# Result tiles summed by halves, row tiles six steps apart, one adapter product four steps later

## The chip, the cores and the metric

The kernel runs on one core of one Trainium2 chip. The metric is the device time of one execution in microseconds (us), lower is better. Times of several executions are given by their median. TensorE (PE) does the matrix products, PEld are its weight loads, VectorE (DVE), ScalarE (ACT) and GpSimd (POOL) do elementwise work, and SyncE (SP) issues all the DMAs that matter here.

## The reference, cut to what matters

Eight sequences of 512 rows, 1024 wide, all float32. The last two matrix products of each sequence, each followed by a layer norm and a residual sum, are what this case is about:

```
x = x + layernorm(attention(layernorm(x)) @ Wo)          # "projection"
x1 = layernorm(x)
y = x1 @ weight.T + bias + (x1 @ A[adapter]) @ B[adapter]  # adapter for some sequences only
x = x + layernorm(y)                                     # "last stage"
```

The adapter product (rank 16, three adapters side by side and masked) is added to y.

## The kernel before, in words

**Products.** Every 512 x 1024 by 1024 x 1024 product is done by a Strassen-Winograd scheme of two levels: seven groups (`GROUPS`, L51) of seven products each (`SUBS`), so 49 products of one sequence. One product is one **step** of the schedule. It is two matmuls of 128x256 (with float32 they show as four records) and takes 0.864 us when nothing is in the way, in the last stage 0.43 us more where an adapter product is added to the same PSUM tile. The sequences are counted q = 0 to 15: 0 to 7 are the projection, 8 to 15 the last stage. So q begins at step base = 49 q, and the stage runs from about 1690 us to the end of the span. The first three groups of q = 0 are done in the stage before.

**The order of work is written by hand.** `at(tick, fn)` puts a piece of work on a step; `run` (L176) goes through a step in this order: work marked "pe", then the product of the step and the drain of the product before it (`fill`, L375), then all other work in the order in which it was put there. Each engine does its instructions strictly in that order. For one q, `plan_right` (L1149) is put down before the sums of result tiles, and those before `plan_rows` (L1181); rows of q - 1 that fall into the steps of q come before all of them.

**A group's drain.** A group's result is one tile of 2 x 512 columns; half j holds the rows of one row tile. In `Group.drain` (L339) ACT copies product P1 (slot 1 of the seven) to `p1`, DVE adds accumulator b to it (`u2`). After P7 (slot 5) DVE runs three adds of 128x256: `p1` plus b, then two result quarters (from accumulators c and d). P2 (slot 6) gives the quarter that completes **half 0**, copied by ACT one step later. P3 of the group is run in slot 2 of the next group, into the same accumulator c, and its drain, one step later, completes **half 1**. So the P3 matmul in slot 2 must wait until the DVE adds that follow P7 have read accumulator c. With the last group of a sequence (steps 42 to 48, result tile `A`), that is: product P7 in step 47, its DVE adds in step 48, and the P3 matmul in step 51, two steps into the next sequence.

**Sums of result tiles.** Tiles c11, c21, c12, c22, U and A are then summed (`combine`, L358). DVE does a whole tile in one instruction (128x1024), POOL does two of 128x512. Before, the steps within a sequence are: 18 c11+=A (DVE), 38 c21+=c12 (POOL), 45 U+=A, 46 c22+=U (DVE), 47 c21+=U (POOL), 48 c12+=c22, 52 c22+=A (DVE).

**Rows.** `plan_rows` takes four row tiles t through their layer norm: load, statistics on DVE, `norm` on ACT, `add_row` on POOL (L1106), store; in the projection also a second layer norm (x1), its transposes on DVE (`turn_x1`, L1115, 0.7 us each) and the store of x1 in DRAM (`store_x1`, eight small DMAs a tile), which is read back eight sequences later.

**Right operands.** `plan_right` loads R11, R21, R12, R22 of the next sequence (SP) and forms T1, T2, T4, T3 in three instructions each (`sum_right`, L275: 128x512, 128x512, 128x768). In the projection all four are POOL's. For q >= 8 T1 and T3 are DVE's; there each R is also differenced (`sub_right`, L263), and `lora_in` (L1135) puts 16 short matmuls per half of the rows on PE, whose result DVE masks (`lora_keep`, L1144).

Of the kernel before, what the change touches and what calls it, by code (L numbers as in the profile page):

```python
# [18 lines left out]
B, S, E = 8, 512, 1024  # L19
# [11 lines left out]
ALL = slice(None)  # L31
# [101 lines left out]
def sandwich_kernel(  # L133
# [15 lines left out]
    nc = tc.nc  # L149
# [43 lines left out]
    def at(tick, fn, kind=None):  # L193
        events[tick].append((kind, fn) if kind else fn)
# [51 lines left out]
    def load_right(pool, q, n):  # L246

        g, h = int(n[1]) - 1, int(n[2]) - 1
        open_right(pool, q, n)
        if q < B:  # L250
            nc.sync.dma_start(out=RX[q, n], in_=attn[q][:, g, h])
            return
        for m in range(4):
            t, k = divmod(m, 2)
            nc.sync.dma_start(
                out=RX[q, n][:, m].rearrange("p c n -> p (c n)").rearrange("p (a m) -> p a m", a=4),
                in_=x1t[q - B][:, 2 * h + t, :, 2 * g + k, :],
            )
# [96 lines left out]
            elif p == "P3":  # L355
                add(self.dest(0, 1), t["u2"], "c")

    def combine(q, out, x, y, eng):  # L358
        for j in (ALL,) if eng is nc.vector else (0, 1):
            eng.tensor_tensor(C[q, out][:, j], C[q, x][:, j], C[q, y][:, j], op=ALU.add)  # L360


# [32 lines left out]
    def stats(key, srcs, step):  # L395
        small = env["small"]
        if step == 0:
            ln[key] = small.tile([P, 2, 6], F32, tag="bnst", name=f"bn_{key}")
        if step < 2:
            nc.vector.bn_stats(ln[key][:, step, :], srcs[step])  # L400
        if step == 1:
            mv = small.tile([P, 2], F32, tag="mv", name=f"mv_{key}")
            nc.vector.bn_aggr(mv, ln[key])
            ln[key] = mv
        if step == 2:
            mv = ln[key]
            sd = small.tile([P, 1], F32, tag="sd", name=f"sd_{key}")
            nc.scalar.activation(sd, mv[:, 1:2], AF.Sqrt, bias=eps, scale=1.0)
            ln[key] = mv, sd
        if step == 3:  # L410
            mv, sd = ln[key]
            rs = small.tile([P, 1], F32, tag="rstd", name=f"rstd_{key}")
            nc.vector.reciprocal(rs, sd)
            nb = small.tile([P, 1], F32, tag="nb", name=f"nb_{key}")
            nc.vector.tensor_scalar(nb, mv[:, 0:1], rs, -1.0, op0=ALU.mult, op1=ALU.mult)
            ln[key] = rs, nb

    def norm(key, dst, src):
        rs, nb = ln[key]
        nc.scalar.activation(dst, src, AF.Identity, bias=nb, scale=rs)  # L420
# [16 lines left out]
    dve, pool = nc.vector, nc.gpsimd  # L437
# [104 lines left out]
    for b in range(B):  # L542
        base = b * N2
# [46 lines left out]
    for n in range(8):  # L590
        base = min(n + 1, B - 1) * N2
# [71 lines left out]
    m = {}  # L663
# [225 lines left out]
    late = {k - (B * N2 + 4): events[k] for k in sorted(events)}  # L889
# [61 lines left out]
    for u in range(UQ + 1):  # L951
        for k in () if u in (0, UQ) else (4, 13, 22, 31) if u in (4, 5, 6) else (18, 26, 34) if u == 1 else (9, 19, 29):
            base = u * N2 + k
# [17 lines left out]
    AHEAD = 3 * NP  # L971
# [28 lines left out]
    for u in range(UQ + 1):  # L1000
        base = u * N2
# [14 lines left out]
        else:  # L1016
# [24 lines left out]
            for k in range(10, 57):  # L1041
                if k in (51, 56):
                    n = {51: "S2", 56: "S4"}[k]
# [14 lines left out]
    with ExitStack() as a:  # L1058
# [26 lines left out]
        def sub_ht(b):  # L1085
            t = hts[b]
            nc.gpsimd.tensor_tensor(t[:, 4:6], t[:, 0:2], t[:, 2:4], op=ALU.subtract)
            nc.gpsimd.tensor_tensor(t[:, 6:9], t[:, 0:6:2], t[:, 1:6:2], op=ALU.subtract)
# [3 lines left out]
        def halves(q, t):  # L1092
            h, j = divmod(t, 2)
            tags = (("c11", "c21"), ("c12", "c22") if q + 1 == NQ else ("c22", "c12"))[h]
            return [C[q, tag][:, j, :] for tag in tags]
# [12 lines left out]
        def store_rows(q, t):  # L1108
            for h, c in enumerate(halves(q, t)):
                dst = x1d[q][:, t, ts(h, HALF)] if q < B else out[q - B, ts(t, P), ts(h, HALF)]  # L1110
                nc.sync.dma_start(out=dst, in_=c)

        def turn_x1(q, t, g):

            nc.vector.transpose(  # L1115
                halves(q, t)[g].rearrange("p (a k n c) -> p k c a n", a=4, k=2, n=32),
                row[q, t][:, ts(g, HALF)].rearrange("p (k c a n) -> p k c a n", k=2, c=2, a=4),
            )

        def store_x1(q, t, g):  # L1120
            for a in range(4):
                nc.sync.dma_start(
                    out=x1t[q][:, t, a, ts(g, 2)].rearrange("(c e) k n -> e c (k n)", e=32),
                    in_=halves(q, t)[g][32 * a : 32 * a + 32].rearrange("e (c m) -> e c m", c=4),
                )
# [23 lines left out]
        def plan_right(q, base):  # L1149

            if q > 1:
                at(base + 6, next_roles)
            for n, k in (("R11", 10), ("R21", 17), ("R12", 24), ("R22", 31)):
                if q == 1 and n != "R22":
                    continue
                at(base + k, lambda n=n: load_right(gp, q, n))
                if q >= B:
                    at(base + k + 4, lambda n=n: sub_right(q, n, nc.gpsimd, slice(0, 3)))
            if q >= B:
                for h, k in ((0, 25), (1, 39)):  # L1160
                    at(base + k, lambda h=h: lora_in(q - B, h), "pe")
                    at(base + k, lambda ph, h=h: lora_keep(q - B, h, ph), "post")
                    for g in range(2):
                        at(base + k, lambda n=f"R{g + 1}{h + 1}": sub_right(q, n, nc.vector if h else nc.gpsimd, slice(3, 4)))
                at(base + 42, lambda: sub_ht(q - B))
            for n, k in (("T1", 40 if q == 1 or q >= B else 38), ("T2", 46 if q >= B else 45), ("T4", 52), ("T3", 63)):
                eng = nc.vector if q >= B and n in ("T1", "T3") else nc.gpsimd
                for m in range(3):
                    at(
                        base + k + (m if eng is nc.vector else 0),  # L1170
                        lambda n=n, m=m, eng=eng: sum_right(gp, q, n, eng, slice(m, m + 1)),
                    )
# [8 lines left out]
        def plan_rows(q, base):  # L1181

            for t in range(NT):
                k = base + 55 + 7 * t
                key = f"{'o' if q < B else 'y'}{q}_{t}"
                at(k, lambda t=t: load_row(q, t))
                for m in range(4):
                    at(k + m + m // 2, lambda t=t, m=m, key=key: stats(key, halves(q, t), m))
                for h in range(2):
                    at(k + 6 + h, lambda t=t, h=h, key=key: norm(key, halves(q, t)[h], halves(q, t)[h]))  # L1190
                    at(k + 8 + h, lambda t=t, h=h: add_row(q, t, h))
                at(k + 14, lambda t=t: store_rows(q, t))
                if q < B:
                    key = f"x{q}_{t}"
                    for m in range(4):
                        at(k + 14 + m + m // 2, lambda t=t, m=m, key=key: stats(key, halves(q, t), m))
                    for h in range(2):
                        at(k + 20 + h, lambda t=t, h=h, key=key: norm(
                            key, row[q, t][:, ts(h, HALF)], halves(q, t)[h]
                        ))  # L1200
                    for g in range(2):
                        at(k + 24 + g, lambda t=t, g=g: turn_x1(q, t, g))
                        at(k + 29 + g, lambda t=t, g=g: store_x1(q, t, g))

        def plan_last(q, base):

# [38 lines left out]
        for q in range(NQ):  # L1245
            base = q * N2
            if q + 1 < NQ:
                plan_right(q + 1, base)
            if q == B - 1:
                plan_left(base)  # L1250
            dve, pool = nc.vector, nc.gpsimd
            for k, e, res, l, r in (
                (18, dve, "c11", "c11", "A"), (38, pool, "c21", "c21", "c12"), (45, dve, "U", "U", "A"),
                (46, dve, "c22", "c22", "U"), (47, pool, "c21", "c21", "U"),
                (48, dve, "c12", "c12", "c22"), (52, dve, "c22", "c22", "A"),
            ) if q + 1 < NQ else (
                (18, dve, "U", "U", "A"), (31, dve, "c12", "c12", "U"), (33, dve, "U", "U", "c22"),
                (34, pool, "c22", "c22", "c12"), (39, pool, "c11", "c11", "A"),
                (45, dve, "c21", "c21", "c12"),
            ):  # L1260
                if base + k >= AHEAD:
                    at(base + k, lambda a=(q, res, l, r, e): combine(*a))
            if q + 1 < NQ:
                plan_rows(q, base)
            else:
                plan_last(q, base)
# [95 lines left out]
```

## Time and profile before

| | |
|---|---|
| median of 3 runs | 2483.34 us (2482.4 to 2485.61) |
| the profiled execution | 2482.47 us, of which the span of the trace is 2480.7 us |
| PE, DVE, POOL, ACT busy | 96%, 72%, 59%, 43% of the span |
| PE waits from 1690 us to the end | 23.8 us in 15 gaps |
| mean granted TensorE clock | 0.987 of full speed |

The page gives averages over stages with different limits, so the stage that is changed is read by itself. Groups of instructions are named by their line, engine, operation and tiles (out<-in); a helper has one line for many uses, so the tile names and shapes tell them apart. A wait "X <- Y" means that X's engine sat idle until Y was done. In the timeline an instruction's duration runs from its start on the engine to its end, so it holds any time in which the engine was held up inside it.

### The profile page before, as it was taken

To read this page: it belongs to the slowest core of one execution; us is meant where nothing else is said; L and a number is where in the kernel's file an instruction comes from. 1 tells how busy PE (TensorE), PEld (TensorE's weight loads), DVE (VectorE), ACT (ScalarE), POOL (GpSimd) and SP (SyncE) were. 2 spreads that over 40 slices of the span, in tenths; PEclk is the share of its full clock that TensorE was granted. 3 is DMA by queue.
4 is the path that set the end of the run, shared out by engine and by line. 5 is a ranking of instruction groups with operands and counts; after the bars stand their busy time and mean duration, and the time that the engine had idled before them with its cause. 6 is when DMAs were issued, how large, how long until landed. Compare 5 with 4: busy or idle time off the path is not lost.

```text
span 2480.7 us, 37119 instructions
## 1 busy us (share of the span) xinstructions
PE 2373.1 (96%) x11936; PEld 1868.7 (75%) x11936; DVE 1791.5 (72%) x3945; ACT 1060.3 (43%) x2685; POOL 1464.1 (59%) x1087
## 2 busy tenths in 40 slices
PE   6999999999999999999999999899999998999997
PEld 4787887886677777777777766458888877888886
DVE  8777767485857759586684856766898987766676
ACT  3323331025555555556555566762434333222223
POOL 3878875204463553736545363326787886777674
PEclk8999999999999999999999999899999999999999
DMA  7697787998899897988989896557778798444433
GB/s 262 197 302 248 243 269 235 346 296 266 269 307 276 256 342 236 326 282 288 333 262 328 265 312 214 169 196 267 230 207 250 201 280 220 126 130 124 115 111 119
DMA packets 505650, 601.82 MB, mean 243 GB/s; under 512 B 198417, under 2 KB 344849, under 8 KB 502898
## 3 DMA queue, kind: packets, MB, share of 16 engines
q1 hardware_dynamic: 505458, 599.46, 76.2%
q8 instruction: 96, 1.57, 0.3%
q14 instruction: 96, 0.79, 0.1%
HBM read 366.55 MB, written 199.23 MB: 228 GB/s over the span
## 4 chain that ended last, share of the span: by engine, by line
PE 66%; DVE 7%; DMA 5%; POOL 2%; ACT 2%; issue 1%; SPq 1%; ACTq 0%; POOLq 0%; DVEq 0%
PE accc_q_P L641 7%; PE accb_q_P L641 7%; PE acca_q_P L641 7%; PE accc_P L320 7%; PE accb_P L320 6%; PE acca_P L320 6%; PE s L752 6%; PE po L832 5%; PE ptp L811 5%; PE accd_P L320 3%; PE accd_q_P L641 3%; DMA attn<-opt 1%; PE ph L1135 1%; DMA R<-x1t 1%; ACT pr L797 1%
## 5 line engine op out<-in xcount | busy, mean ns | idle before, releaser
L783 ACT ACTIVATE pr<-pr,nm 128x128 f32<-128x128 f32 (+3 forms) x512 | 280.9, 550 | 171.9 <-DVE nm L773 171.7
L797 ACT ACTIVATE pr<-pr,rs 128x128 f32<-128x128 f32 (+2 forms) x500 | 245.2, 549 | 117.2 <-DVE rs L791 117.1
L773 DVE CUSTOM_DVE_ANT_0 pr<-s,mask 128x128 f32<-128x128 f32 (+3 forms) x512 | 224.4, 485 | 43.5 <-PE s L752 40.9
L641 PE MATMUL acca_q_P<-xs,ls 128*128 128x256 f32 x896 | 217.3, 385 | 0.8 <-issue 0.8
L641 PE MATMUL accc_q_P<-xs,ls 128*128 128x256 f32 x896 | 217.7, 386 | 0.0
L1106 POOL TENSOR_TENSOR c<-c,row 128x512 f32<-128x512 f32 x120 | 158.3, 1328 | 99.7 <-ACT c L420 84.0
L641 PE MATMUL accb_q_P<-xs,ls 128*128 128x256 f32 x896 | 216.3, 384 | 0.8 <-DVE u_q_P L116 0.8
L641 PEld LDWEIGHTS acca_q_P<-xs,ls 128*128 128x128 f32 x896 | 165.3, 190 | 49.9 <-issue 20.4
L641 PEld LDWEIGHTS accc_q_P<-xs,ls 128*128 128x128 f32 x896 | 165.8, 190 | 48.4 <-issue 20.8
L752 PE MATMUL s<-qk 64*128 64x128 f32 (+3 forms) x1024 | 194.5, 474 | 6.0 <-DVE nm L773 5.5
L641 PEld LDWEIGHTS accb_q_P<-xs,ls 128*128 128x128 f32 x896 | 165.4, 190 | 44.9 <-issue 6.9
L811 PE MATMUL ptp<-ident,pr 128*128 128x128 f32 x1280 | 178.4, 278 | 11.8 <-ACT pr L797 5.6
L275 POOL TENSOR_TENSOR T<-R,T 128x512 f32<-128x512 f32 (+1 forms) x96 | 174.0, 1839 | 24.0 <-PE accc_P L320 17.3
L811 PEld LDWEIGHTS ptp<-ident,pr 128*128 128x128 f32 x1280 | 147.2, 142 | 44.4 <-ACT pr L797 17.1
L567 POOL TENSOR_TENSOR wc_g<-wc_g 128x256 f32<-128x256 f32 (+1 forms) x120 | 125.9, 1068 | 80.0 <-DMA wc_g<-in_wqk_dram 76.7
L832 PE MATMUL po<-pT,v 128*64 128x512 f32 (+3 forms) x1024 | 158.1, 447 | 9.8 <-ACT pT L826 9.8
L832 PEld LDWEIGHTS po<-pT,v 128*64 128x64 f32 x1024 | 72.9, 138 | 102.3 <-issue 65.5
L683 POOL TENSOR_TENSOR B_q<-B_q,m 128x1024 f32<-128x1024 f32 x14 | 34.9, 2496 | 189.0 <-DVE B_q L680 189.0
L752 PEld LDWEIGHTS s<-qk 64*128 64x128 f32 x1024 | 73.2, 187 | 47.5 <-issue 28.7
L641 PE MATMUL accd_q_P<-xs,ls 128*128 128x256 f32 x448 | 108.7, 385 | 0.0
L826 DVE COPY pT<-ptp 128x384 f32<-128x384 f32 (+1 forms) x129 | 78.7, 615 | 38.1 <-PE ptp L811 38.1
L567 POOL TENSOR_TENSOR wc_wo<-wc_wo 128x256 f32<-128x256 f32 (+1 forms) x64 | 66.0, 1047 | 64.0 <-DMA wc_wo<-in_wo_dram 50.1
(1107 smaller groups left out, 5710.1 us busy)
## 6 DMA issues: line engine op xcount, KB each, us to landing
ls<-wqk SPq DMA_DIRECT2D x392, 256.0 KB, 5.1
xs<-xop SPq DMA_DIRECT2D x392, 256.0 KB, 5.3
R<-attn SPq DMA_DIRECT2D x32, 896.0 KB, 6.3
wqk<-wc_g SPq DMA_DIRECT2D x16, 1568.0 KB, 9.4
x<-in_x_dram SPq DMA_DIRECT2D x32, 512.0 KB, 9.6
v<-vd SPq DMA_DIRECT2D x64, 256.0 KB, 5.4
attn<-ops SPq DMA_DIRECT2D x16, 1024.0 KB, 8.1
row<-in_x_dram SPq DMA_DIRECT2D x32, 512.0 KB, 4.2
```

Source lines behind the costliest of these rows:

```text
L275: eng.tensor_tensor(RX[q, n][:, c], RX[q, x][:, c], RX[q, y][:, c], op=ALU.subtract)
L320: nc.tensor.matmul(acc, lhsT=stays, rhs=moving, start=(first and k == 0), stop=True, skip_group_check=True,)
L567: eng.tensor_tensor(out, x, y, op=op)
L641: nc.tensor.matmul(acc[:, :, w, :], lhsT=ls[:, k, w, :], rhs=xs_[:, :, k, :], start=(first and w == 0 and k == 0), stop=True, skip_group_c ...
L752: nc.tensor.matmul(ps[:, j, at : at + L], lhsT=qT[r, qb], rhs=kT[r, : qb + 1], start=True, stop=True,)
L773: nc.vector.tensor_tensor_reduce(out=v[:, j, :], in0=self.ps[qb][:, j, :], in1=work2["mask"][:, S - L :], scale=-1.0 / HD**0.5, scalar=3.0e38,
L783: nc.scalar.activation(v[:, j, :], v[:, j, :], AF.Exp, bias=nm[:, j : j + 1], scale=-1.0, accum_out=sm[:, j : j + 1],)
L797: nc.scalar.mul(v, v, rs[:, j : j + 1])
L811: nc.tensor.transpose(pt[:, n, :], self.pr[qb][:, j, ts(kb, P)], ident)
L826: copy(self.pT[j][:, : qb + 1, ts(qb, P)], self.pt[j][:, : qb + 1, :])
L832: nc.tensor.matmul(po[j * HD : (j + 1) * HD, kb * P :], lhsT=self.v[:, kb, ts(j, HD)], rhs=self.pT[j][:, kb, kb * P :], start=(kb == 0), s ...
L1106: nc.gpsimd.tensor_tensor(c, c, row[q, t][:, ts(h, HALF)], op=ALU.add)
```

## The change

Three things are done; the number of products and their order are the same.

1. The sums of result tiles of q = 0 to 14 are done by halves, each at its own step. Seven sums become fourteen instructions; on DVE 128x512 twice takes the place of 128x1024 once. c12+=c22 now comes in steps 44 and 47, ahead of the drain of step 48, and the first half of c21+=U ahead of T2 in POOL's order.
2. Row tile t starts at step base + 53 + 6 t, before at base + 55 + 7 t, and what comes from the store on is one step nearer to the row tile's start.
3. Only for the operands of q = 8 (in q = 7's steps): the second `lora_in` with its `lora_keep`, two `sub_right` and `sub_ht` is four steps later, T1 at step 45 and no longer 40, T2 at 48 and no longer 46.

```diff
-    def combine(q, out, x, y, eng):
-        for j in (ALL,) if eng is nc.vector else (0, 1):
+    def combine(q, out, x, y, eng, j=None):
+        for j in (j,) if j is not None else (ALL,) if eng is nc.vector else (0, 1):
             eng.tensor_tensor(C[q, out][:, j], C[q, x][:, j], C[q, y][:, j], op=ALU.add)
...
-                for h, k in ((0, 25), (1, 39)):
+                late = 4 * (q == B)
+                for h, k in ((0, 25), (1, 39 + late)):
...
-                at(base + 42, lambda: sub_ht(q - B))
-            for n, k in (("T1", 40 if q == 1 or q >= B else 38), ("T2", 46 if q >= B else 45), ("T4", 52), ("T3", 63)):
+                at(base + 42 + late, lambda: sub_ht(q - B))
+            for n, k in (("T1", 45 if q == B else 40 if q == 1 or q > B else 38), ("T2", 48 if q == B else 46 if q > B else 45), ("T4", 52), ("T3", 63)):
...
-                k = base + 55 + 7 * t
+                k = base + 53 + 6 * t
...
-                at(k + 14, lambda t=t: store_rows(q, t))
+                at(k + 13, lambda t=t: store_rows(q, t))
...
-                        at(k + 24 + g, lambda t=t, g=g: turn_x1(q, t, g))
-                        at(k + 29 + g, lambda t=t, g=g: store_x1(q, t, g))
+                        at(k + 23 + g, lambda t=t, g=g: turn_x1(q, t, g))
+                        at(k + 28 + g, lambda t=t, g=g: store_x1(q, t, g))
...
-            for k, e, res, l, r in (
-                (18, dve, "c11", "c11", "A"), (38, pool, "c21", "c21", "c12"), (45, dve, "U", "U", "A"),
-                (46, dve, "c22", "c22", "U"), (47, pool, "c21", "c21", "U"),
-                (48, dve, "c12", "c12", "c22"), (52, dve, "c22", "c22", "A"),
+            for ks, e, res, l, r in (
+                ((14, 18), dve, "c11", "c11", "A"), ((36, 38), pool, "c21", "c21", "c12"),
+                ((42, 45), dve, "U", "U", "A"), ((43, 46), dve, "c22", "c22", "U"),
+                ((44, 47), pool, "c21", "c21", "U"), ((44, 47), dve, "c12", "c12", "c22"),
+                ((50, 53), dve, "c22", "c22", "A"),
```

The steps of the second layer norm's statistics and `norm` move by the same one step. The sums of the last sequence (q = 15) keep their steps and sizes.

## The prediction on record

> **What bounds it.** I read the page first: PE is busy 96% of the span. So only PE's gaps can be won, and the stage from 1690 us on was asked by itself for what PE waits for (total us, times, longest):
>
> ```profile
> PE accc_P L320 <- DVE A L342: 14.5, 9, 1.9
> PE ph L1135 <- DMA R<-x1t: 4.4, 2, 3.7
> PE accb_P L320 <- DVE u_P L342: 2.6, 2, 2.1
> PE accc_P L320 <- DVE U L342: 1.3, 1, 1.3
> PE accb_P L320 <- POOL T L275: 1.0, 1, 1.0
> ```
>
> The first row is the P3 matmul of step 51, held by the DVE adds of step 48. The timeline places it: 1.91, 1.91, 1.91, 1.05, 1.92, 1.91 us at the ends of q = 1 to 6 (1754 to 1978 us), 1.25 at q = 7, the rest at q = 8 and in the last sequence. From q = 9 to 14 PE has no gap. A second cost hides in the windows cut at those matmuls (length, busy times, then granted clock):
>
> ```profile
> 1753.90:1800.10 46.20, 44.26 (x196) 38.34 (x196) 40.51 (x89) 18.65 (x38) 36.32 (x25) 0.96 0.81 236
> 1800.10:1844.70 44.60, 42.72 (x196) 37.07 (x196) 40.42 (x89) 18.75 (x38) 36.74 (x25) 1.00 0.70 211
> ```
>
> After the gap at 1754 the clock is halved for a while: 4% of 46.2 us, about 1.8 us lost. It happens after two of the five gaps of 1.9 us (q = 1 and 6), after the 2.07 us one (q = 7) and after the 3.7 us one, not after shorter ones.
>
> **Why DVE is late at step 48.** The timeline of the end of q = 5, DVE, POOL and PE:
>
> ```profile
> 1928.06 1.27 POOL L275 TENSOR_TENSOR T<-R,T 128x512 f32<-128x512 f32 x1
> 1928.13 2.28 DVE L360 TENSOR_TENSOR U<-U,A 128x1024 f32<-128x1024 f32 x1
> ...
> 1929.29 2.25 POOL L275 TENSOR_TENSOR T<-R,T 128x512 f32<-128x512 f32 x1
> ...
> 1930.45 2.17 DVE L360 TENSOR_TENSOR c<-c,U 128x1024 f32<-128x1024 f32 x1
> ...
> 1931.50 2.79 POOL L275 TENSOR_TENSOR T<-R,T 128x768 f32<-128x768 f32 x1
> 1932.55 0.41 DVE L342 TENSOR_TENSOR p_P<-accb_P,p_P 128x256 f32<-128x256 f32 x1
> 1932.99 0.42 DVE L342 TENSOR_TENSOR A<-accc_P,p_P 128x256 f32<-128x256 f32 x1
> ...
> 1933.47 0.92 PE L320 MATMUL accc_P<-wo_S,R 128*128 128x256 f32 x3 [1.92 <-DVE A L342]
> ```
>
> Read the ends. POOL's first T ends at 1929.33; DVE's U, begun at 1928.13, ends 1.08 us after that. POOL's next T, begun at 1929.29, ends at 1931.54, 1.13 us after U. c22 ends 1.08 us after that T. Alone, the DVE sum takes 1.22 us (q = 0) and the POOL one 1.27. So a DVE sum of two SBUF operands and a POOL sum **exclude each other and take turns**: each DVE instruction lets one POOL instruction pass, 1.13 us (128x512) or 1.68 (128x768). DVE's adds from PSUM (0.41), statistics (0.68) and transposes (0.70) don't lengthen. A DVE instruction of half size pays the same turn, as a 128x512 one shows:
>
> ```profile
> 2018.50 1.45 POOL L1106 TENSOR_TENSOR c<-c,row 128x512 f32<-128x512 f32 x1
> ...
> 2018.75 1.75 DVE L275 TENSOR_TENSOR T<-R,R 128x512 f32<-128x512 f32 x1
> ```
>
> 1.75 us: 1.20 until POOL's ended (2019.95), then 0.55. Alone it takes 0.65 (2045.33 us).
>
> **Part 1, the halves.** Before step 48's adds there were two big DVE sums (U, c22); now there are six half ones (U, c22, c12 twice), as c12+=c22 moves in front of that drain. What each lets pass decides.
>
> End of q = 5 in its own times: step 38 at 1920.17, 42 at 1923.62, 51 at 1931.4. Row tile 3's add_row is now at steps 30 and 31 and out of POOL's way, so T1 starts at 1920.4 (before 1921.36), and its third instruction ends at 1924.65. Then, in turns (0.53 for a DVE half, 1.13 or 1.68 for POOL): U half 0 to 1925.2, POOL's c21 half 1 to 1926.3, c22 half 0 to 1926.85, c21+=U half 0 to 1928.0, c12 half 0 to 1928.5, T2 to 1929.65, U half 1 to 1930.2, T2 to 1931.3, c22 half 1 to 1931.85, T2's 768 columns to 1933.55, c12 half 1 to 1934.1, two adds of step 48 (0.9) to 1935.0. The adds of steps 44 and 45 and two transposes (0.34 + 0.31 + 1.26) fit into the turns. PE wanted 1931.4: **a gap of 3.6 us where there was 1.92**. If T1 starts 1.2 us later, one POOL instruction takes the place of another, with the same end. After such a gap I count 0.1 for the restart and 0.8 times the halved clock's 1.8: 5.0 us a boundary. Six of them 30.0; before, 10.6 of gaps, 0.6 of restarts, two halved clocks 3.6, together 14.8. **+15.2.** From below: without turns (six at 0.62) DVE would be done at 1930.9, and the whole 14.8 is won.
>
> **The last stage** had no gap but little room. End of q = 11:
>
> ```profile
> 2252.45 2.17 DVE L360 TENSOR_TENSOR c<-c,U 128x1024 f32<-128x1024 f32 x1
> ...
> 2254.99 0.42 DVE L342 TENSOR_TENSOR A<-accc_P,p_P 128x256 f32<-128x256 f32 x1
> ...
> 2256.11 0.81 PE L320 MATMUL accc_P<-wf_S,R 128*128 128x256 f32 x3
> ```
>
> The adds are done 0.7 us before PE wants them. DVE's T1 ends at 2250.2, as before; then U half 0 to 2250.85 and c22 half 0 to 2251.45 without a turn, POOL's c21+=U half 0 to 2252.6, c12 half 0 to 2253.15, T2 to 2254.3, U half 1 to 2254.85, T2 to 2256.0, c22 half 1 to 2256.5, T2's 768 to 2258.2, c12 half 1 to 2258.75, the adds to 2259.65: **a gap of 3.5 us that was not there**, again 5.0 with its clock. q = 9 to 14: **+30.0**; q = 8, which had 2.9 of gaps there: **+2.1**. From below: without turns the adds end at about 2255.5, and nothing is lost.
>
> q = 0 has no rows in these steps, but T1 of q = 1 at step 40 stands in U's way: by the same turns 1.5 us of gap are new, and the 1.0 us for POOL's T4 goes, as half a c21 sum moves into an idle time of POOL's: **+0.5**. c11 in halves at steps 14 and 18 now meets two row tiles' statistics (steps 16 to 18): from 0 to 0.6 us in six sequences, **+1**. c22+=A (50, 53) comes behind the adds; DVE has room until step 55, so nothing; without that cover 0.5 per boundary.
>
> **Part 2, the rows.** No instruction is added; a row tile's ten DMAs, ACT's norms and POOL's adds stay as many, and ACT (some 18.7 of 45 us) and POOL have the room. What moves is SP's queue: the last eight x1 stores of q = 7 come at q = 8's steps 1 and 2, before at 7 and 8, where they stood right in front of R11's load for q = 9 (stores until 2043.1 us, load 2043.2). From 2036 to 2064 us the DMA queue is 96% busy, and PE waits 3.7 us for R21, with a halved clock behind it. Those stores held SP for 4.7 us (1.91 + 2.75), more than 3.7. Between nothing and 5.5 us won; I take all of it, as 4.7 is over 3.7: **-5.5**.
>
> **Part 3.** In q = 7's steps 0.67 us of waiting for R22 go. But `lora_keep` (0.54), two differences (0.41 alone) and T1's three (0.65, 0.65, 0.95 alone) move from steps 39 to 42 into 43 to 47, behind `lora_in` (2.0 us of PE), in front of the same drain. In us from step 42: the masks can't start before 2.95, c22 half 0 ends at 6.45, the add PE needs for step 47 at 6.8 (0.5 late), then, in turns, T1, U and c22's second halves, transposes and c12 to 15.75, the adds 16.6; step 51 wants them at 10.2. 0.5 + 6.4 + 1.8 = 8.7, before 0.67 + 2.07 + 1.25 + 1.8 + 0.2 = 6.0: **+2.7**, from -4 (turns missed) to +6 (R22 late too).
>
> **Sum:** 15.2 + 30.0 + 2.1 + 0.5 + 1.0 - 5.5 + 2.7 = +46.0 on the profiled execution's 2482.47 (span 2480.7 and 1.8 around it; 0.9 under the median): **2528.5 us**.
>
> [...]
>
> **Rivals.** *The halves pass without turns* (10%): the mechanism is the port's order at steps 42 to 47. For it speaks that U half 0 starts three steps earlier and that the first two halves of the last stage meet no POOL work; against it that T2 must run in just these steps (its buffer is free at step 45). With no turn the projection's chain ends 0.5 us before PE wants it. It decides from the second or third turn on: 2.4 us of delay bring the old gap of 1.92 back. Price: -14.8 - 2.9 - 5.5 - 2 (q = 7) - 1.0 = -26: **2456 us**. *The boundaries stay as they are* (5%): half of the turns are missed, DVE's earlier start pays for the others, and only R21's wait goes: **2477 us**. The forecast has 85%.
>
> **Range.** Own case: no halved clock -20, the last stage's gaps 2 us shorter -14; upward the clock always halved +5, R21's wait stays +5.5, c11 +2.6, q = 7 +3.3. 2494 to 2545, a little more for sums of them: 2492 to 2546 holds nearly all of 85%. A measurement tells some 0.2% (5 us) from no change; half of the second rival lies over that. Faster 13%, same 3%, slower 84%.
>
> **What would show it.** PE's row accc_P <- DVE A with some 15 entries and 45 to 55 us, longest 3 to 6.5, also in q = 9 to 14; DVE's L360 as 128x512, about 1.6 us in the mean though 0.65 alone; POOL's T2 between them one by one; the clock under 1.00 in most sequences of the stage; no wait for R<-x1t over 1 us. I am wrong if DVE's halves are near 0.7 us, or if two of them run with a POOL sum waiting.

## The result, and the profile after

| us | before | after |
|---|---|---|
| median of 4 runs each | 2482.87 (2478.72 to 2485.61) | 2548.95 (2546.74 to 2550.47) |
| the profiled execution, and its span | 2482.47, 2480.7 | 2548.88, 2547.1 |
| PE waits from 1690 us to the end | 23.8 | 60.3 |
| mean granted clock | 0.987 | 0.976 |

The changed kernel is slower by 2.7%: the ratio is 1.0272, 95% interval 1.0257 to 1.0288. The forecast was 2528.5 with a range of 2492 to 2546, so the sign and the place were foreseen and the size was not: 66.4 us in the profiles where 46.0 were forecast.

What PE waits for, from 1690 us to the end of the kernel after (total us, times, longest):

```profile
PE accc_P L320 <- DVE A L342: 53.0, 16, 5.9
PE accb_P L320 <- DVE u_P L342: 4.8, 8, 1.9
PE ph L1135 <- DMA R<-x1t: 1.4, 1, 1.4
```

The row that stood at 14.5 us with 9 entries has 53.0 with 16. That is the P3 matmul of step 51, now held at every boundary: 2.74 us at q = 0, 3.51 to 3.53 at q = 1 to 6, 5.90 at q = 7, 3.12 at q = 8, 3.11 at q = 9 to 14, and the last sequence's 1.49 as before. The row of R<-x1t falls from 4.4 to 1.4.

The end of q = 5 in the timeline of the kernel after, some lines of DVE, POOL and PE:

```profile
1951.54 0.81 DVE L360 TENSOR_TENSOR U<-U,A 128x512 f32<-128x512 f32 x1
...
1952.89 1.13 DVE L360 TENSOR_TENSOR c<-c,U 128x512 f32<-128x512 f32 x1
1953.43 2.25 POOL L275 TENSOR_TENSOR T<-R,T 128x768 f32<-128x768 f32 x1
1954.13 2.10 DVE L360 TENSOR_TENSOR c<-c,c 128x512 f32<-128x512 f32 x1
1956.16 0.41 DVE L342 TENSOR_TENSOR p_P<-accb_P,p_P 128x256 f32<-128x256 f32 x1
1956.60 0.42 DVE L342 TENSOR_TENSOR A<-accc_P,p_P 128x256 f32<-128x256 f32 x1
1957.08 0.80 PE L320 MATMUL accc_P<-wo_S,R 128*128 128x256 f32 x1 [3.53 <-DVE A L342]
```

Read the ends again. POOL's 768 columns of T2 start at 1953.43, when the second half of c22 is under way, and end at 1955.68. The second half of c12 starts on DVE at 1954.13 and ends at 1956.23, 0.55 us after POOL. It takes 2.10 us, of which 0.55 lie behind POOL's end (a half sum right after, at 1957.46 us, takes 0.69 in all). Only then come the two adds for which PE waits. This is the order that the forecast had, and its last turn.

The rest of the price is mostly in the clock. Two of the windows cut at the matmuls of step 51 (length, busy times, clock), one of the projection and one of the last stage, where before the clock was 1.00:

```profile
1858.20:1908.20 50.00, 45.82 (x197) 38.95 (x197) 44.07 (x94) 18.51 (x38) 35.65 (x25) 0.94 0.68 201
2185.00:2243.60 58.60, 55.50 (x260) 47.32 (x260) 40.63 (x78) 11.89 (x26) 38.95 (x33) 0.97 0.39 108
```

And the 3.4 us pieces around the gap at 1957 us:

```profile
1952.50:1955.90 3.40, 1.05 (x5) 0.57 (x3) 3.29 (x3) 0.30 (x1) 3.40 (x3) 1.00 0.67 134
1955.90:1959.30 3.40, 2.22 (x5) 1.85 (x6) 2.55 (x7) 0.37 (x1) 1.46 (x2) 0.50 0.90 264
1959.30:1962.70 3.40, 3.40 (x9) 2.69 (x8) 3.18 (x5) 0.00 (x0) 3.40 (x3) 0.50 0.16 65
1962.70:1966.10 3.40, 3.40 (x17) 2.96 (x17) 1.56 (x5) 0.57 (x2) 1.30 (x1) 1.00 0.00 0
```

For two whole pieces the clock is 0.50, and a PE that is busy all the time gets through 9 records where it gets through 17 in the next. Cut into such pieces, the stage after has fifteen halved stretches, ten of one piece and five of two; before it had four. Fourteen of the fifteen boundaries have one (only q = 8 has none), and the fifteenth follows a wait of 1.90 us at step 40 of q = 7.

### The profile page after: what moved, and what is told of

Its sections match the earlier page's. It is cut to its first block, busy times and chain, and to the rows that moved or that the text cites. A ratio compares the mean times of both kernels' runs of the same rounds, so it can differ in the third digit from the quotient of the medians.

```text
span 2547.1 us, 37198 instructions
## 1 busy us (share of the span) xinstructions
PE 2400.1 (94%) x11936; PEld 1883.4 (74%) x11936; DVE 1844.1 (72%) x4019; ACT 1056.6 (41%) x2685; POOL 1455.4 (57%) x1087
## 3 DMA queue, kind: packets, MB, share of 16 engines
q8 instruction: 96, 1.57, 0.3%
## 4 chain that ended last, share of the span: by engine, by line
PE 52%; DVE 15%; DMA 7%; POOL 4%; issue 3%; ACT 3%; SPq 1%; DVEq 0%; ACTq 0%; POOLq 0%
PE accc_q_P L641 6%; PE acca_q_P L641 6%; PE accb_q_P L641 6%; PE accc_P L320 5%; PE s L752 5%; PE po L832 5%; PE ptp L811 4%; DVE c L360 4%; PE accb_P L320 4%; PE acca_P L320 3%; PE accd_q_P L641 3%; PE accd_P L320 2%; DMA attn<-opt 1%; PE ph L1135 1%; DVE U L360 1%
## 5 line engine op out<-in xcount | busy, mean ns | idle before, releaser
L773 DVE CUSTOM_DVE_ANT_0 pr<-s,mask 128x128 f32<-128x128 f32 (+3 forms) x512 | 224.2, 484 | 41.1 <-PE s L752 39.0
L275 POOL TENSOR_TENSOR T<-R,T 128x512 f32<-128x512 f32 (+1 forms) x96 | 163.9, 1733 | 29.0 <-PE accc_P L320 13.4
L263 POOL TENSOR_TENSOR R<-R 128x256 f32<-128x256 f32 x96 | 77.6, 809 | 67.7 <-DMA R<-x1t 55.0
```

The costliest lines, as they stand in the source:

```text
L275: eng.tensor_tensor(RX[q, n][:, c], RX[q, x][:, c], RX[q, y][:, c], op=ALU.subtract)
L773: nc.vector.tensor_tensor_reduce(out=v[:, j, :], in0=self.ps[qb][:, j, :], in1=work2["mask"][:, S - L :], scale=-1.0 / HD**0.5, scalar=3.0e38,
```

## The experiments

My theory stayed that of the prediction: DVE's sums of two SBUF operands and POOL's sums take turns (before, at the end of q = 5, each ended 1.08 to 1.13 us after the other's), so work put in front of the drain of step 48 costs its own time and POOL's beside it. Its rivals were that the halving itself costs (twice as many instructions, twice as many turns), that another part of the change costs, and that the clock takes more than I gave it. Each ratio is to the kernel before, with its 95% interval.

**One part at a time: e1_halves, e2_rows, e3_late.** Each is the kernel before with one of the three parts of the diff, as printed above.

> The kernel before with part 1 alone (sums by halves at the changed steps; rows and adapter product as before). Theory (turns between DVE's half sums and POOL's sums hold up the adds of step 48): nearly all of the +66 us, 2535 to 2550 us, gaps of 3.4 to 3.6 us at the ends of q = 1 to 6 and of 3.0 to 3.2 at q = 9 to 14, each with a halved clock behind it. Rival (the rows, now packed, and the late adapter product make the time, a half sum costs only its start): 2483 to 2490 us, gaps under 2 us.

> The kernel before with part 2 alone (row tiles six steps apart). Theory: the gaps at the ends of q = 1 to 6 stay near 1.9 us, some 0.5 us at step 33 are new in each, the wait of 3.7 us for R21 at q = 8 gets shorter or goes: 2476 to 2487 us. Rival (the rows make the time): over 2510 us.

> The kernel before with part 3 alone (second adapter product of q = 8 four steps later, T1 at 45, T2 at 48). Theory: q = 7 alone changes, the gap at its end grows from 1.25 to 3 to 5 us, the wait for R22 goes: 2482 to 2489 us. Rival (it makes a good part of the time): over 2495 us.

- e1_halves: 2559.47 us, ratio 1.0308 (1.0290 to 1.0327), over the expectation. Its gap at q = 1 to 6 is 5.2 us, with 1.38 more at step 47: with the rows at their old steps, statistics on DVE stand right in front of the half sums (at the end of q = 3 until 1846.3 us, the first half of U begins at 1846.48), and POOL's `add_row` right in front of its c21 sum and T1.
- e2_rows: 2486.78 us, ratio 1.0016 (1.0005 to 1.0027): the time as expected, close to no change, but not the waits (below).
- e3_late: 2482.29 us, ratio 0.9994 (0.9982 to 1.0006): no change in the time. In its trace the gap at the end of q = 7 is 5.38 us, the wait for R22 is gone, and the wait for R21 falls from 3.70 to 1.02.

So part 1 alone makes all of the loss, and the other two, alone worth some +4 and -1 us, take some 10 us off in its company (2559.47 to 2548.95). For e2_rows the waits from 1690 us on say why alone it wins nothing:

```profile
PE accc_P L320 <- DVE A L342: 13.2, 10, 2.5
PE ph L1135 <- DMA R<-x1t: 6.0, 2, 4.5
PE accc_P L320 <- DVE c L342: 3.8, 6, 0.7
PE accb_P L320 <- DVE u_P L342: 3.6, 7, 0.6
```

At q = 1 to 6 the gap at step 51 falls from 1.9 to about 1.0, but the packed rows make new waits in the middle of a sequence, the third and fourth rows (0.62 at step 23 and 0.51 at step 33). And the wait for R21, which I had laid to the stores' place in SP's queue, is still there: 4.5 us. It is gone in the kernel after and in e1_halves, 1.02 us in e3_late, and back at 2.57 in e10_fill. What takes it away isn't shown.

**Are there turns at all: e5_memset.** The kernel after, with POOL's T2 (for q from 1) and c21+=U as memsets: as many POOL instructions, at the same places, that read nothing. (Its result is therefore another one; only its time is of use.)

```diff
+            if q > 0 and n == "T2":
+                eng.memset(RX[q, n][:, c], 0.0)
...
+            if q >= 0 and out == "c21" and y == "U":
+                eng.memset(C[q, out][:, j], 0.0)
```

> The changed kernel, but POOL's T2 (q from 1 on) and its c21+=U are memsets of the same tiles: as many POOL instructions at the same places, which read nothing (T2 and those two tiles are zero, so the result is another). Theory (POOL sums that read SBUF and DVE sums of two SBUF operands take turns): DVE's half sums of U and c22's second halves and c12 fall to about 0.65 us; no gap at the ends of q = 9 to 14, 0.5 to 1 us at q = 1 to 6, where c21 and T1 still take turns: 2475 to 2492 us. Rival (any POOL instruction, or the number of DVE instructions, holds DVE up): within 10 us of 2549.

Measured 2478.63 us, ratio 0.9982 (0.9973 to 0.9992), as expected. The whole loss is gone, with all six half sums still ahead of the drain: 0.73 us of gap at q = 1 to 6, none at q = 9 to 14, no halved stretch there. The groups of DVE's c12 halves, in the kernel after and in this one (where the line is 366), with busy time and mean ns, and the memsets of T2:

```profile
L360 DVE TENSOR_TENSOR c<-c,c 128x512 f32<-128x512 f32 x30 | 50.0, 1666 | 1.6
```

```profile
L366 DVE TENSOR_TENSOR c<-c,c 128x512 f32<-128x512 f32 x30 | 20.6, 685 | 1.6
...
L276 POOL MEMSET T<- 128x512 f32 x30 | 14.8, 522 | 14.7 <-PE accc_P L323 14.7
```

1666 ns with a reading POOL beside it, 685 with a writing one. A memset is also shorter (0.52 us, where a sum on POOL alone takes 1.27), but a shorter neighbour alone would leave turns of 0.5 us, and c12's halves show none. (The halves of U and c22 keep 752 and 947 ns in the mean, as some of them still meet POOL's T1 and c21+=c12, which read.)

**The halving or the place: e6_whole, e8_c12_front, e4_c12_back, e9_two_halved.** Four runs separate "six halves instead of two wholes" from "c12 in front of the drain".

e6_whole is the kernel after with DVE's sums whole again, each at the step of its second half. (POOL's first half of c21+=U then comes ahead of DVE's U, so that half is summed from U before A is in it, and the result is another one.)

```diff
-                ((42, 45), dve, "U", "U", "A"), ((43, 46), dve, "c22", "c22", "U"),
-                ((44, 47), pool, "c21", "c21", "U"), ((44, 47), dve, "c12", "c12", "c22"),
+                ((45,), dve, "U", "U", "A"), ((46,), dve, "c22", "c22", "U"),
+                ((44, 47), pool, "c21", "c21", "U"), ((47,), dve, "c12", "c12", "c22"),
```

> The changed kernel, but DVE's sums are whole again, at the step of the second half (c11 18, U 45, c22 46, c12 47, c22+=A 53); POOL's halves, rows and adapter product as changed. So c12 stays in front of the drain, and three DVE instructions stand there and not six. Theory (each DVE instruction lets one POOL instruction pass): gaps 3.5 to some 2.5 us at q = 1 to 6 and 3.1 to 0.2 to 1.0 at q = 9 to 14, the halved clock goes with the latter: 2500 to 2520 us. Rival (c12 in front of the drain is the cost, the halves are not): 2540 us or more.

Measured 2543.34 us, ratio 1.0241 (1.0228 to 1.0255), far over what I expected of it. The gaps are 3.77 at q = 1 to 6 and 3.02 at q = 9 to 14, close to those with halves (3.5 and 3.1), and there are fifteen halved stretches again. So with c12 in front of the drain it makes little difference whether six halves or three whole sums stand there.

e8_c12_front is the kernel before with one number changed:

```diff
-                (48, dve, "c12", "c12", "c22"), (52, dve, "c22", "c22", "A"),
+                (47, dve, "c12", "c12", "c22"), (52, dve, "c22", "c22", "A"),
```

> The kernel before with one number changed: c12+=c22, whole, at step 47 and not 48, so it stands in front of the drain of step 48 and not behind it. Theory as it is after the run with whole sums (the cost is c12's place: its turn is the one behind T2's 768 columns): gaps 1.9 to 4.5 to 5 us at q = 1 to 6, new ones of 2 to 3 at q = 9 to 14, halved clocks with them, 2525 to 2550 us. Rival (the halves are the cost): 2483 to 2495 us.

Measured 2529.08 us, ratio 1.0192 (1.0175 to 1.0209), as expected. Its timeline at the end of a sequence of the projection:

```profile
1841.69 2.29 DVE L360 TENSOR_TENSOR U<-U,A 128x1024 f32<-128x1024 f32 x1
1844.02 2.17 DVE L360 TENSOR_TENSOR c<-c,U 128x1024 f32<-128x1024 f32 x1
1846.30 2.63 DVE L360 TENSOR_TENSOR c<-c,c 128x1024 f32<-128x1024 f32 x1
...
1849.30 0.42 DVE L342 TENSOR_TENSOR A<-accc_P,p_P 128x256 f32<-128x256 f32 x1
1849.78 0.79 PE L320 MATMUL accc_P<-wo_S,R 128*128 128x256 f32 x1 [4.67 <-DVE A L342]
```

Three whole sums stand in front of the adds where there were two. The third takes 2.63 us and the gap grows by 2.75, from 1.92 to 4.67. At q = 9 to 14 there are new gaps of 1.95 us, and after four of the six a halved stretch. This one number costs 47.8 us, where the whole change costs 66.

e4_c12_back is the reverse: the kernel after, with c12's halves behind the drain.

```diff
-                ((44, 47), pool, "c21", "c21", "U"), ((44, 47), dve, "c12", "c12", "c22"),
+                ((44, 47), pool, "c21", "c21", "U"), ((48, 51), dve, "c12", "c12", "c22"),
```

> The changed kernel, but c12+=c22 in halves at steps 48 and 51, behind the drain of step 48 as before; all else as changed. Theory: the two turns of c12's halves (among them the one behind T2's 768 columns) leave the way to the adds: gaps 3.5 to 1.3 us in the projection and 3.1 to 1.3 in the last stage, too short to halve the clock as a rule, so some 13 x 3.5 us less than the changed kernel: 2495 to 2515 us. Rival (rows): within 10 us of 2549.

Measured 2509.72 us, ratio 1.0104 (1.0087 to 1.0122), as expected: 39 us come back. In the projection the gap at step 51 is 0.86, but the half sums now stand in front of other adds: 0.58 us for an add u_P, 1.48 at step 58, and smaller ones. In the last stage the gap moves to step 58 (1.44). Some 27 us over the kernel before are left.

e9_two_halved is the kernel before with U and c22+=U in halves, at steps 42 and 45, 43 and 46, and all else whole and in its place.

> The kernel before with only U+=A (steps 42 and 45) and c22+=U (43 and 46) in halves; c11, c21, c12 (whole, at 48), c22+=A, rows and adapter product as before. Theory (c12's place is the cost; halves pay twice the turns, but start three steps earlier): gaps of 1.7 to 2.2 us at q = 1 to 6, none at q = 9 to 14, 2477 to 2492 us. Rival (the halves are the cost: two turns more in front of the adds): gaps of 3 to 4 us at q = 1 to 6 and 1.5 to 2.5 at q = 9 to 14, 2510 to 2535 us.

Measured 2502.69 us, ratio 1.0084 (1.0064 to 1.0104): I had expected at most 2492, and neither side's range holds it. At the ends of q = 1 to 6 the halves are no loss (the gap is 1.33 where it was 1.91). The last stage pays, and the end of q = 7, at a place that I had not costed; the timeline of the last stage there, DVE and PE:

```profile
2207.10 1.76 DVE L360 TENSOR_TENSOR U<-U,A 128x512 f32<-128x512 f32 x1
2208.89 1.63 DVE L360 TENSOR_TENSOR c<-c,U 128x512 f32<-128x512 f32 x1
2210.45 0.41 DVE L342 TENSOR_TENSOR u_P<-accb_P,p_P 128x256 f32<-128x256 f32 x1
2210.91 1.14 PE L320 MATMUL accb_P<-wf_S,R 128*128 128x256 f32 x4 [1.98 <-DVE u_P L342]
```

The first halves of U and c22 come in front of the add u_P of step 44, which the product of step 47 needs. POOL is in T2, so both pay a turn and PE waits 1.98 us, with a halved clock behind it here and in three of the other five sequences. So halving alone, with c12 left behind the drain, costs some 21 us. In the kernel after this wait doesn't come: POOL's first half of c21+=U comes ahead of T2, waits for U, and so keeps POOL still while U half 0 and c22 half 0 pass in 0.68 and 0.69 us.

**How much is the clock: e10_fill.** The kernel after, with twelve small matmuls into a tile that nobody reads, ahead of the P3 matmul of step 51 of q = 0 to 14. They give PE something to do in the gap.

```diff
+        def fill_gap():
+            t = ps_t.tile([P, NH, P], F32, tag="tp", name="fill")
+            for n in range(12):
+                nc.tensor.matmul(t[:, n % NH, :], lhsT=ident, rhs=ident, start=True, stop=True)
+            return t
...
+                at(base + 51, fill_gap, "pe")
```

> The changed kernel, and at step 51 of q = 0 to 14, ahead of the P3 matmul that waits, twelve matmuls of 128x128 into a PSUM tile that nobody reads (some 2.6 us of PE at full clock). They lie inside the gaps of 2.7 to 5.9 us, so DVE's way to the adds is as long as before and the gaps shrink to what the fill leaves. Theory (the halved clock comes from PE standing still for 2.7 us or more, and costs some 20 to 25 us of the changed kernel): most of the 15 stretches at half clock go, 2522 to 2537 us. Rival (the clock is halved for another reason, or costs little): 2545 to 2560 us.

Measured 2521.47 us, ratio 1.0164 (1.0141 to 1.0187), half a microsecond under the range I gave for it. A boundary in its timeline, then the window of a last stage sequence:

```profile
2277.06 2.84 PE L1152 MATMUL fill<-ident 128*128 128x128 f32 x24
2280.34 1.14 PE L320 MATMUL accc_P<-wf_S,R 128*128 128x256 f32 x4 [0.43 <-DVE A L342]
```

```profile
2222.00:2280.30 58.30, 57.46 (x291) 49.64 (x289) 42.24 (x81) 11.89 (x26) 39.31 (x33) 1.00 0.38 109
```

2.84 us of idle matmuls and a 0.43 us wait fill the gap of 3.11: the product starts no earlier, and yet the kernel is 27.5 us faster. The clock is 1.00, and of fifteen halved stretches one is left. PE's waits and the fill are together longer than the waits were before it (26.2 + 42.6 us against 60.3), so at least 27 us of the change's 66 were the halved clock: PE's busy time x (1 - clock), over pieces of 3.41 us from 1690 us on, falls from 29.5 to 1.7.

**A version that beats both: e7_behind.** If what stands in front of the drain is the price, c22+=U can go behind it too. The kernel before, with two numbers changed:

```diff
-                (46, dve, "c22", "c22", "U"), (47, pool, "c21", "c21", "U"),
-                (48, dve, "c12", "c12", "c22"), (52, dve, "c22", "c22", "A"),
+                (48, dve, "c22", "c22", "U"), (47, pool, "c21", "c21", "U"),
+                (51, dve, "c12", "c12", "c22"), (52, dve, "c22", "c22", "A"),
```

> The kernel before, with whole sums and its rows, but c22+=U moved behind the drain of step 48 (at step 48) and c12+=c22 to step 51; U 45, c21+=U 47, c22+=A 52 as before. Theory: one DVE sum and one turn in front of the adds and not two, so the gaps at the ends of q = 1 to 6 (1.9 us) go, with their halved clocks, and those of q = 7 and 8 shrink; c12 and c22+=A come nearer to the drain of step 55, up to 0.7 us of gap there: 2463 to 2476 us. Rival (the gaps are not set by what stands in front of the adds): within 4 us of before.

Measured 2474.23 us, ratio 0.9963 (0.9949 to 0.9976), as expected: 8 us, a small gain but clear of the noise. Its waits from 1690 us on:

```profile
PE accc_P L320 <- DVE A L342: 8.8, 10, 1.5
PE ph L1135 <- DMA R<-x1t: 6.9, 3, 4.0
```

The gap at step 51 is gone. In the projection 0.9 us comes back at step 58, where another add now stands behind c12. U can't follow behind the drain, since the adds of step 48 write tile A, which U reads; that would take a second buffer and wasn't tried.

## Why the prediction went as it did

**The account,** from the two profiles, with the terms of the sum sorted in the same way:

| us | forecast | measured |
|---|---|---|
| time in which PE waits | +33 | +36.5 |
| halved clock | +13 | +23 to +27 |
| the rest | 0 | 3 to 7 |
| sum | +46 | +66.4 |

The forecast's clock is 13 boundaries of 0.8 x 1.8 and one of 1.8, less the four of 1.8 before. The measured one is the loss over pieces of 3.41 us from 1690 us on: PE's busy time x (1 - clock) is 6.3 before and 29.5 after, and with the whole length of each piece it is some 7 and 34. The rest holds 1.0 us that arose before the stage, and, as I suppose, the restarts (at full clock the four records of a product take 1.13 us behind a gap of 1.91 and 1.03 without one).

**What held.** *What bounds it*: PE's gaps at step 51 and the clock behind them; the waits elsewhere are few us. *The turns*: e5_memset takes the read operands from POOL, and the loss is gone (2478.63 us). *The gap sizes*: 3.6 forecast and 3.53 measured for the projection, 3.5 and 3.11 for the last stage, 6.4 and 5.9 for q = 7. In the last stage the first halves of U and c22 pass without a turn, as forecast (0.68 and 0.69 us).

**The step that failed** is "After such a gap I count 0.1 for the restart and 0.8 times the halved clock's 1.8". 1.8 was read off one gap of 1.91 us, and the factor off a handful. Here gaps of 2.7 us and over halved the clock at 14 boundaries of 15, and at five of them for two pieces of 3.4 us and not one, which costs about twice as much. The term should have been about 2 us a boundary for certain, where I had 1.44. It was worst in the projection: from the end of q = 1 to that of q = 6 a sequence is 4.5 us longer (246.7 us for five where it was 224.2), forecast 2.5; in the last stage 5.7 (59.2 where it was 53.5), forecast 5.0. The range failed with it: "upward the clock always halved +5" holds no stretch of double length, so 2546 lay 3 us short.

**What the records say of the clock.** The prediction left open why two of the five gaps of 1.9 us halved the clock and three didn't. The records answer it. In the traces of both kernels every change of the clock lies a whole number of 3.413 us from the first (within 0.01 us), so all halved stretches of a run lie on one grid. Cut on it, the end of q = 1 before (first two lines) and that of q = 2 (third line), gaps of 1.91 us both, look like this:

```profile
1750.75:1754.17 3.42, 1.51 (x7) 1.00 (x7) 3.35 (x6) 0.37 (x1) 3.42 (x2) 1.00 0.56 135
1754.17:1757.58 3.41, 3.41 (x9) 2.70 (x9) 3.41 (x6) 0.37 (x1) 3.41 (x3) 0.50 0.67 127
...
1798.54:1801.96 3.42, 1.85 (x9) 1.64 (x10) 3.38 (x6) 0.37 (x1) 3.42 (x2) 1.00 0.50 152
```

The gap of q = 1 lies within one piece, PE is busy for 1.51 us of it, and the next piece is at half clock. The gap of q = 2 lies across a border, 1.85 us are left in the emptier piece, and the next one is at 1.00. Count in each piece PE's busy time x the clock. The traces of both kernels have 470 pieces from 1690 us on (without the last 20 us). After all 21 with less than 1.47 us comes a piece at half clock; after none of the 441 with 1.60 or more; the 8 in between go both ways. So in this stage of these two traces the piece behind one with less than about 1.5 us of such work was at half clock. (Over the whole traces, with the other matmuls of the earlier stages, it is less sharp: 40 of 40, and 4 of 1403.) The two other odd cases agree with it. The 3.12 us at q = 8 fall across a border, 1.57 us of work in one piece and 2.14 in the other, and halve nothing. And in the four pieces at 1957 us above, the one from 1955.90 has 2.22 us of busy time at half clock, which counts 1.11, and the next is halved too. An estimate from these numbers: a gap must come near 3.41 - 1.5 = 1.9 us to halve the clock at all (the shortest seen to is 1.86, at 1712 us in e2_rows), and over twice that, 3.8, it always would. PE needn't have stood still for a whole piece: gaps of 2.74 us (q = 0) and 3.11 us (q = 9 to 14) had a halved piece behind them, seven of seven. That is read from the records; e10_fill agrees with it, but no run shifted a gap on the grid with all else the same.

**Smaller sizes.** q = 0 has a gap of 2.74 where I had 1.5, with a halved clock that I left out: about 3 us. The packed rows make a wait of 0.50 us at step 33 of each of q = 2 to 6, 2.5 us in all: the add u_P of step 30 comes late because DVE waits 0.70 us for ACT's copy to `p1`, and on ACT that copy stands behind `norm`s of 0.80 us. I had costed part 2 by how busy SP, ACT and POOL are, and not by what stands in front of what. At q = 7 the 0.5 us at step 47 didn't come; instead PE waits 1.90 us at step 40 (that group's u_P stands behind statistics that wait 2.30 us for POOL's `add_row`), and 1.43 us at step 25 for R21 of q = 8, against the sign "no wait for R<-x1t over 1 us". With the 5.90 at step 51 that is 2.3 us more of waits than forecast, and three halved pieces where I had one. The sum itself takes 5.0 us for a boundary of the projection where its terms (3.6 + 0.1 + 1.44) give 5.14, 0.8 us in all. The +1 for c11 didn't come, as the waits for an add to c are 0.5 us in all.

**Right in sum, wrong in cause.** *Part 2, -5.5*: R21's wait did go, but not by the stores' place alone, as e2_rows keeps it at 4.5 us. What part 2 does here is to clear the way for the half sums: e1_halves, without it and part 3, has gaps of 5.2 us and is 10.5 us slower than the whole change. How much of that 10.5 belongs to part 3 wasn't measured; part 3 touches q = 7 alone, so it can be little of it. *Part 1*: I wrote "now there are six half ones" and summed six turns. The sum is right, but three whole sums give nearly the same gap (e6_whole), and c12's place is the larger part of the 66 us: 48 when it alone is moved (e8_c12_front), 39 when it alone is put back (e4_c12_back). The main cause is that a third sum stands in front of the drain, more than that the sums are halved. Halving isn't free either: it costs 21 us with c12 left behind the drain (e9_two_halved), mostly at step 47, and 5.6 us with c12 in front (2548.95 against 2543.34 in e6_whole).

**Rivals.** "The halves pass without turns" (2456) is refuted by the kernel after itself, and e5_memset shows what it would have needed: a POOL that doesn't read (c12's halves 685 ns, where they were 1666). The prediction laid it to "the port's order"; no run shows a port, only sums that end one after the other (before, q = 5: 1.08 to 1.13 us apart). "The boundaries stay as they are" (2477) fails on the same lines.

**Open.** The last 3 to 7 us of the account aren't settled, nor what decides in the narrow band around 1.5 us of work (1.49 to 1.59) where both clocks follow.

## What to carry to other kernels

Before a piece of work is moved, list what stands in front of the add or copy that TensorE waits for, in each engine's own order; one sum moved from behind such a drain to in front of it cost 48 us here, and moving one from in front of it to behind won 8. Count DVE sums of two SBUF operands together with the POOL sums beside them, as if the two were one engine: here c12's half sums took 1666 ns beside POOL sums and 685 beside memsets. And price a gap of TensorE at its length plus a halved clock behind it, with the double stretch in the range: here a gap of 3.1 us cost 5.7. The shortest gap seen with a halved piece behind it in this stage is 1.86 us.

## What the hardware showed that I had not expected

- POOL's memsets, which only write, didn't hold DVE up here: half sums of 685 ns beside memsets, 1666 ns beside sums.
- In both traces the clock changed only at borders of pieces of 3.41 us. In this stage a piece was at half clock after one with less than 1.47 us of PE's work (21 of 21), and never after one with 1.60 or more (0 of 441), so gaps of 1.91 us halved one piece or none, and gaps of 3.5 us one or two.
- Matmuls without a use were worth their place in a gap here: 2.84 us of them at each of 15 boundaries made the kernel 27.5 us faster.
